# The last row tile's 20 rows on three groups of partitions, three chunks' products issued together

## The chip, the cores and the metric

The kernel runs on one core of one Trainium2 chip. The metric is device time in microseconds (us), lower is better. A core has TensorE (PE in the profile; PEld are its weight loads), VectorE (DVE), ScalarE (ACT), GpSimd (POOL), the queue engine SyncE (SP) and 16 DMA engines. PE contracts over partitions: a product `matmul(acc, lhsT, rhs)` sums over the partitions of lhsT and rhs and writes the result to PSUM.

## The reference

Four graph layers work on 2708 nodes with 128 features each and one dense adjacency matrix of 2708 x 2708 (fp32, 29 MB), with a residual and a layer norm after each:

```python
# layer 0: neighbourhood mean, similarity of z, the 4 nearest are added to A
d = 1 / sqrt(sum(A, -1));  z = leaky_relu((d * (A @ (d * x))) @ W1 + b1)
S = exp(-dist(z, z) / 2), kept for the 4 nearest of each row;  A2 = S + A
x = layernorm(x + (d2 * (A2 @ (d2 * x))) @ W2 + b2)
# layer 1: attention
XW = x @ W;  den = exp(leaky_relu(s_row[:, None] + s_col[None, :]));  num = A @ den
x = layernorm(x + A @ ((den / num) @ XW))
# layer 2: normalised adjacency
x = layernorm(x + (dn * (A @ (dn * x))) @ W.T + b)
# layer 3: own features beside the neighbours' sum
x = layernorm(x + relu(concat([x, A @ x]) @ W.T + b))
```

A enters six times as the large operand. Each time the kernel passes over all of it, with the nodes as the contraction.

## The kernel before

A is stored transposed. A pass computes `acc[:, k] = sum over j of lhsT[j, :] * adjT[j, k]`. The 2708 rows j make T = 22 row tiles of 128; the last, tile 21 (`FULL`), has `LAST` = 20 rows. The columns k make C = 6 chunks of 512, 512, 512, 512, 384 and 276. Of the row tiles, S = 16 are streamed from memory in every pass, four to a panel, through a pool of three buffers; six (16 to 21) stay in SBUF in `res`. A chunk's sum is one PSUM bank.

Five of the six passes run through this helper (the operands are called y2, lc, mixed, y3 and xs; y2 and y3 share a buffer that the profile calls y):

```python
    def by_panels(weights, done, tick=None, ready=(), first=None, behind=None):
        ready = list(ready)
        for c in range(C):
            w = cw[c]
            acc = acc_tile()
            for n, i in enumerate(first if first and c == 0 else range(T)):
                if i < S:
                    if i % 4 == 0:
                        ...                                  # load the next panel
                    src = part[:, i % 4, :w]
                else:
                    src = res[: pw[i], i - S, cols[c]]       # pw[21] is 20
                lhsT = weights(i)
                nc.tensor.matmul(                            # L181 in the profile
                    acc[: lhsT.shape[-1], :w], lhsT=lhsT, rhs=src, start=(n == 0), stop=(n == T - 1 and tick is None)
                )
                if n == T - 1:
                    done(c, acc)
                if tick is not None:
                    tick()
```

`done` evacuates the sum and does the chunk's small work (bias, residual, norm, the next operand). The y2 pass also calls `tick`, which issues other work at given counts of products: the kernel gathers each node's four nearest rows with indirect DMAs on GpSimd (88 of them, `got`), sums them on VectorE (`near_sum`), and adds the sums to acc by a product with the identity (L580).

The first pass is written out on its own, since it runs while A is first read:

```python
        def add(c, i, src, first=False, last=False):
            nc.tensor.matmul(                                # L364 in the profile
                accs[c][:, : cw[c]], lhsT=y[: pw[i], i, :], rhs=src[: pw[i], : cw[c]], start=first, stop=last
            )
        ...
        def add_group(c, g, part, last=False):
            for i in chunk_tiles[g]:                         # group 5 holds tiles 19, 20 and 21
                add(c, i, part[:, i % 4, :] if i < S else resident(c, i), i == 0, last and i == chunk_tiles[g][-1])
                due.tick()
        ...
            rest(3, 4)
            add_group(*wait)                                 # chunk 5, group 5
            finish(5)
            rest(3, 5, True)
            finish(3)
            for c in (2, 1, 0): ...                          # each ends with its group 5
```

The order of the passes: the first pass (operand y), the similarity of z (PE and VectorE), the y2 pass, a ranking of the attention scores, the lc pass (its lhsT has 86 columns), the attention itself (L1008 and L937, rows gathered by indirect DMA into the panels' buffers), and then the passes on mixed, y3 and xs. In front of the xs pass stands a loop over the 22 tiles with a transpose (L1061) and a product with layer 3's own-feature weights (L1065); the scheduler weaves it into that pass's first chunk.

PSUM pools: six acc buffers up to the similarity stage, three after it.

Of the kernel before, what the change touches and what calls it, by code (L numbers as in the profile page):

```python
# [16 lines left out]
P = 128  # L17
# [33 lines left out]
def kernel(  # L51
# [16 lines left out]
    nc = tc.nc  # L68
    N, D = x.shape
    assert D == P  # L70
    T = (N + P - 1) // P
# [13 lines left out]
    cw = [b - a for a, b in zip(starts, [*starts[1:], N])]  # L85
    cols = [slice(a, a + w) for a, w in zip(starts, cw)]

    chunk_tiles = [range(a // P, (a + w + P - 1) // P) for a, w in zip(starts, cw)]

    const = ctx.enter_context(tc.tile_pool(name="const", bufs=1))  # L90
# [57 lines left out]
    def load_panel(g, c, pool=stream):  # L148
# [5 lines left out]
        )  # L154
        return s

    def by_panels(weights, done, tick=None, ready=(), first=None, behind=None):

        ready = list(ready)
        for c in range(C):
            w = cw[c]
            acc = acc_tile()
            for n, i in enumerate(first if first and c == 0 else range(T)):
                if i < S:
                    if i % 4 == 0:
                        if ready:
                            part = ready.pop(0)  # L170
                        elif behind is not None:
                            with tc.issue_after(behind):
                                part = load_panel(i // 4, c)
                            behind = None
                        else:
                            part = load_panel(i // 4, c)
                    src = part[:, i % 4, :w]
                else:
                    src = res[: pw[i], i - S, cols[c]]
                lhsT = weights(i)  # L180
                nc.tensor.matmul(  # L181
                    acc[: lhsT.shape[-1], :w], lhsT=lhsT, rhs=src, start=(n == 0), stop=(n == T - 1 and tick is None)
                )
                if n == T - 1:
                    done(c, acc)
                if tick is not None:
                    tick()

# [5 lines left out]
        return done  # L194

    def rows_of(y):
        return lambda i: y[: pw[i], i, :]

    def inv_sqrt(dst, src):
        nc.scalar.activation(dst, src, AF.Sqrt)  # L200
# [100 lines left out]
    with tc.tile_pool(name="knn", bufs=1) as knn:  # L301
# [59 lines left out]
        accs = [acc_tile() for _ in range(C)]  # L361

        def add(c, i, src, first=False, last=False):
            nc.tensor.matmul(  # L364
                accs[c][:, : cw[c]], lhsT=y[: pw[i], i, :], rhs=src[: pw[i], : cw[c]], start=first, stop=last
            )

        def resident(c, i):
            return res[:, i - S, cols[c]]
# [1 line left out]
        due = Due()  # L371

        def add_group(c, g, part, last=False):
            for i in chunk_tiles[g]:
                add(c, i, part[:, i % 4, :] if i < S else resident(c, i), i == 0, last and i == chunk_tiles[g][-1])
                due.tick()

        def finish(c):
# [12 lines left out]
        with (  # L391
            tc.tile_pool(name="load", bufs=4) as load,
            tc.tile_pool(name="degp", bufs=2) as degp,
            tc.manual_schedule(engines={nc.tensor.engine}),
        ):
            wait = None
            for c in range(C):
                w = cw[c]
                load_x(chunk_tiles[c])
                parts = [load_panel(g, c, load if g < G - 1 else stream) for g in range(G)]  # L400
                nc.sync.dma_start(
                    res[:, : FULL - S, cols[c]],
                    adjT[S * P : FULL * P, cols[c]].rearrange("(t p) k -> p t k", p=P),
                )
                if LAST:
                    nc.sync.dma_start(res[:LAST, FULL - S, cols[c]], adjT[FULL * P :, cols[c]])
                both = degp.tile([P, 2, CW], F32, tag="both", name="both")
                nc.vector.tensor_add(both[:, :, :w], parts[0][:, :2, :w], parts[0][:, 2:, :w])
                more = [part[:, n : n + 2, :w] for part in parts[1:] for n in (0, 2)]
                more += [res[:, n : n + 2, cols[c]] for n in range(0, RES, 2)]  # L410
                for m in more:
                    nc.vector.tensor_add(both[:, :, :w], both[:, :, :w], m)
                nc.vector.tensor_add(both[:, 0, :w], both[:, 0, :w], both[:, 1, :w])

                for g in range(min(c, G)):
                    add_group(c, g, parts[g])
                    if wait is not None:
                        add_group(*wait)
                        wait = None
                if c == C - 1:  # L420
                    add_group(c, G, None)
                ts = chunk_tiles[c]
                dps = mis_tile()
                for k, t in enumerate(ts):
                    nc.tensor.matmul(
                        dps[: pw[t], k : k + 1], lhsT=both[:, 0, k * P : k * P + pw[t]], rhs=ones, start=True, stop=True
                    )
                full = sum(pw[t] == P for t in ts)
                t0, t1 = ts[0], ts[-1] + 1
                nc.vector.tensor_copy(deg[:, t0 : t0 + full], dps[:, :full])  # L430
                if t0 + full < t1:
                    nc.vector.tensor_copy(deg[:LAST, t0 + full : t1], dps[:LAST, full : full + 1])
                inv_sqrt(dinv[:, t0:t1], deg[:, t0:t1])
                scale_rows(y, xs, dinv, ts)
                wait = (c, c, parts[c] if c < G else None, c == C - 1)
                if c == C - 2:
                    w1_sb = load_const(w1, D, "w1")
                    w2_sb = load_const(w2, D, "w2")
                    wa_sb = load_const(w_att, D, "w_att")
                    wl_sb = load_const(w_lap_t, D, "w_lap")  # L440
                    wx_sb = load_const(w_cat_t[:D, :], D, "w_cat_x")
                    wh_sb = load_const(w_cat_t[D:, :], D, "w_cat_h")
                    b1_sb = load_rows(b1, D, "b1")
                    b2_sb = load_rows(b2, D, "b2")
                    bl_sb = load_rows(b_lap, D, "b_lap")
                    bc_sb = load_rows(b_cat, D, "b_cat")
                    a_sb = load_rows(a_att, 2 * D, "a_att")


            def rest(c, g, end=False):  # L450
                add_group(c, g, load_panel(g, c) if g < G else None, end)

            assert (C, G) == (6, 4)
            rest(3, 4)
            add_group(*wait)
            finish(5)
            rest(3, 5, True)
            finish(3)
            for c in (2, 1, 0):
                for g in range(c + 1, C):  # L460
                    if (c, g) == (1, 4):
                        rest(4, 5, True)
                        finish(4)
                    rest(c, g, g == C - 1)
                finish(c)
            due.flush()
# [15 lines left out]
        def weigh(ts):  # L482
# [14 lines left out]
            if t1 < T:  # L497
                nc.gpsimd.tensor_mul(  # L498
                    y2[:, t0:t1, :], xs[:, t0:t1, :], d2inv[:, t0:t1, None].to_broadcast([P, t1 - t0, D])
                )  # L500
            else:
                scale_rows(y2, xs, d2inv, ts)
            full = min(t1, FULL)
            queue = nc.gpsimd if t1 < T else nc.sync
            ins = queue.dma_start(
# [180 lines left out]
        at(near_at[t], sum_near, t)  # L686

    def end_pass2(c, acc):
        n = max(T * (c + 1), near_at[chunk_tiles[c][-1]] + 3)
        ts = chunk_tiles[c]  # L690

        def finish():
# [42 lines left out]

    with tc.manual_schedule(engines={nc.tensor.engine, nc.vector.engine, nc.scalar.engine}):
        by_panels(
            rows_of(y2), end_pass2, due.tick, ready, [*range(S - 4), *range(S, T - 2), *range(S - 4, S), T - 2, T - 1], written
        )
        due.flush()  # L740
    late.close()
# [7 lines left out]
    with tc.tile_pool(name="rank", bufs=1) as rank:  # L749
# [72 lines left out]
        with tc.manual_schedule(engines={nc.vector.engine}):  # L822
            for t0, t1 in ((0, 4), (4, half_t), (half_t, T)):
# [10 lines left out]
                for side, (op, v) in enumerate(((ALU.is_gt, e_r), (ALU.is_lt, f_r))):  # L834
                    sel = rtile([half_t, NB], "sel", BF16)
                    nc.vector.tensor_tensor(sel[:, :n, :], blk_g, iota_g, op=op)
                    nc.vector.tensor_mul(lc[:, t0:t1, :, side], sel[:, :n, :], v[:, t0:t1, None].to_broadcast([P, n, NB]))  # L837

        for t0, t1 in halves:
            n = t1 - t0  # L840
# [75 lines left out]
            if c == 3:  # L916
                listed()

        by_panels(lambda i: lc[: pw[i], i, :, :].rearrange("p b s -> p (b s)"), end_carry)
        gb = on_all("gb", r_row)  # L920

    def mix(w, q, num, col, haccs, pool):
# [97 lines left out]
    for t in range(T):  # L1020
        p = pw[t]
        pt = mis_tile()
        nc.tensor.transpose(pt[:p, :D], mT[:, t * P : t * P + p], ident)  # L1023
        nc.vector.tensor_scalar_mul(mixed[:p, t, :], pt[:p, :D], f_out[:p, t : t + 1])


    nc.vector.tensor_scalar_add(dinv, deg, DEG_EPS)
# [3 lines left out]
    def end_layer1(c, ts):  # L1031
# [5 lines left out]
        normalize(ts, xs)  # L1037
        for t in ts:
            nc.scalar.mul(y3[: pw[t], t, :], xs[: pw[t], t, :], dinv[: pw[t], t : t + 1])
            nc.gpsimd.tensor_add(xs[: pw[t], t, :], xs[: pw[t], t, :], bl_sb[: pw[t]])  # L1040

    by_panels(rows_of(mixed), into_hT(end_layer1))
# [4 lines left out]
    def end_layer2(c, ts):  # L1047
        for t in ts:
# [3 lines left out]
                xs[:p, t, :], po[:p, :D], dinv[:p, t : t + 1], xs[:p, t, :], op0=ALU.mult, op1=ALU.add  # L1052
            )
        normalize(ts, xs)

    by_panels(rows_of(y3), into_hT(end_layer2))

# [61 lines left out]
```

## Time and profile before

| | |
|---|---|
| time, median of 3 runs | 1134.08 us (1127.51 to 1134.82) |
| span of the profiled run | 1132.0 us |
| instructions | 10737 |
| DMA | 193.89 MB, mean 171 GB/s |

The page gives the busy time of each engine, the span in 40 slices, and groups of instructions. A group's row reads: line, engine, operation, output <- inputs, partitions contracted * output partitions, size, count, busy time and mean length, idle time before. The products of the 20 rows are groups of their own when shapes are kept apart:

```profile
L181 PE MATMUL acc<-res,y 20*128 20x512 f32 x16 | 9.0, 640 | 0.0
L364 PE MATMUL acc<-res,y 20*128 20x512 f32 x8 | 4.5, 640 | 0.0
L181 PE MATMUL acc<-res,mixed 20*128 20x512 f32 x8 | 4.5, 640 | 0.0
L181 PE MATMUL acc<-res,xs 20*128 20x512 f32 x8 | 4.5, 640 | 0.0
L181 PE MATMUL acc<-res,lc 20*86 20x512 f32 x8 | 4.3, 622 | 0.0
```

One fp32 product leaves two records, so x8 are the four chunks of 512 columns of one pass. Records overlap, since a product's end is modelled: what a product takes is read from one start to the next, not from the mean length.

### The profile page before, as it was taken

What the parts mean: (1) busy time and instruction counts of PE and PEld (TensorE: products, weight loads), DVE (VectorE), ACT (ScalarE), POOL (GpSimd) and SP (SyncE); (2) the same over time, 40 slices, a digit from 0 to 9 for tenths busy, and PEclk for the clock granted to TensorE, in tenths of its full rate; (3) what the DMA queues carried; (4) which work ended last, traced back from release to release, by engine and by line L of the source; (5) the groups of instructions that cost most, each with busy time, mean ns of one, the idle gap of its engine ahead of it and who ended that gap; (6) DMA issues with size and microseconds to landing.
All of it is one profiled execution on the core that took longest, in us unless ns stands there. A gap on an engine that the chain in (4) does not pass through costs nothing.

```text
span 1132.0 us, 10737 instructions
## 1 busy us (share of the span) xinstructions
PE 1061.9 (94%) x3495; PEld 496.7 (44%) x3495; DVE 643.0 (57%) x1381; ACT 302.9 (27%) x557; POOL 300.4 (27%) x296
## 2 busy tenths in 40 slices
PE   0899999999999994999899999998999999999997
PEld 0346444444344563333433333333444644565444
DVE  5985439999726678502189999998311211223132
ACT  0000135555302344000065666664100100011000
POOL 4000000000377772773255655561010100000000
PEclk9999999999999996999999999999999999999999
DMA  9996330000386660696635534554475776565743
GB/s 346 335 321 224 112 111 1 1 0 1 121 281 201 208 205 26 195 294 226 206 109 151 172 104 119 161 174 151 150 237 180 219 226 220 166 212 168 250 157 112
DMA packets 110246, 193.89 MB, mean 171 GB/s; under 512 B 14157, under 2 KB 47107, under 8 KB 109927
## 3 DMA queue, kind: packets, MB, share of 16 engines
q1 hardware_dynamic: 91046, 151.12, 40.7%
q0 software_dynamic: 19136, 42.01, 12.1%
q8 instruction: 29, 0.48, 0.2%
q14 instruction: 35, 0.28, 0.1%
HBM read 217.20 MB, written 4.30 MB: 196 GB/s over the span
## 4 chain that ended last, share of the span: by engine, by line
PE 36%; issue 6%; POOL 4%; DMA 3%; DVE 1%; ACT 0%; POOLq 0%; DVEq 0%
PE acc L181 26%; PE hacc L937 4%; PE num L1008 4%; POOL rows L995 4%; DMA rows<-in_adjT,slot_i 2%; DMA part<-in_adjT 1%; PE mis L231 1%; DMA rows<-carry 0%; PE mis L1065 0%; PE mis L1023 0%; PE mis L1061 0%; POOLq L995 0%; PE mis L1035 0%; DVE err L931 0%; ACT mT L1013 0%
## 5 line engine op out<-in xcount | busy, mean ns | idle before, releaser
L181 PE MATMUL acc<-part,y 128*128 128x512 f32 (+2 forms) x384 | 155.9, 548 | 2.2 <-DMA part<-in_adjT 1.7
L995 POOL DMA_INDIRECT rows<-in_adjT,slot_i x86 | 120.4, 1400 | 107.6 <-PE num L1008 79.7
L1008 PE MATMUL num<-rows,lw 128*64 128x512 f32 (+2 forms) x516 | 117.1, 558 | 5.3 <-DMA rows<-carry 2.1
L937 PE MATMUL hacc<-err,xws 128*128 128x512 f32 (+3 forms) x264 | 112.1, 561 | 2.2 <-DVE err L932 1.8
L535 PE MATMUL acc<-zT,z 128*128 128x512 f32 (+4 forms) x264 | 108.6, 558 | 0.0
L563 POOL DMA_INDIRECT got<-y_rows,where x88 | 93.9, 1067 | 29.6 <-issue 10.1
L181 PEld LDWEIGHTS acc<-part,y 128*128 128x128 f32 x384 | 69.3, 190 | 67.3 <-issue 57.5
L930 DVE TENSOR_TENSOR err<-inv,num 128x1024 f32<-128x1024 f32 (+1 forms) x88 | 74.3, 855 | 26.1 <-DMA rows<-in_adjT,slot_i 20.0
L926 ACT ACTIVATE inv<-num 128x1024 f32<-128x1024 f32 (+1 forms) x88 | 64.4, 735 | 86.9 <-PE num L1008 84.3
L536 ACT COPY key<-acc 128x512 f32<-128x512 f32 (+3 forms) x132 | 70.3, 535 | 59.6 <-issue 29.8
L364 PE MATMUL acc<-part,y 128*128 128x512 f32 (+2 forms) x192 | 82.5, 582 | 2.3 <-DVE y L205 2.2
L937 PEld LDWEIGHTS hacc<-err,xws 128*128 128x128 f32 (+1 forms) x264 | 46.5, 189 | 79.7 <-issue 42.3
L181 PE MATMUL acc<-part,lc 128*86 128x512 f32 (+2 forms) x192 | 76.5, 554 | 2.5 <-DVE lc L837 2.5
L181 PE MATMUL acc<-part,xs 128*128 128x512 f32 (+2 forms) x192 | 77.9, 546 | 0.3 <-DMA part<-in_adjT 0.3
L932 DVE SCALAR_TENSOR_TENSOR err<-gb,g_inv,err 128x1024 f32<-128x1024 f32 (+1 forms) x88 | 77.1, 917 | 0.0
L498 POOL TENSOR_TENSOR y<-xs,d2inv 128x2176 f32<-128x2176 f32 (+1 forms) x2 | 4.6, 2324 | 271.7 <-ACT d2inv L496 271.6
L181 PE MATMUL acc<-part,mixed 128*128 128x512 f32 (+2 forms) x192 | 75.6, 546 | 0.2 <-DMA part<-in_adjT 0.2
L535 PEld LDWEIGHTS acc<-zT,z 128*128 128x128 f32 (+1 forms) x264 | 47.5, 188 | 55.4 <-issue 50.1
L931 DVE SCALAR_TENSOR_TENSOR err<-err,inv 128x1024 f32<-128x1024 f32 (+1 forms) x88 | 71.8, 857 | 0.0
L192 ACT COPY hT<-acc 128x512 f32<-128x512 f32 (+2 forms) x18 | 9.6, 536 | 231.0 <-PE acc L181 231.0
L537 DVE MAX8 near<-key 128x8 f32<-128x2708 f32 (+1 forms) x22 | 65.5, 2979 | 4.8 <-ACT key L536 4.8
L927 ACT ACTIVATE inv<-inv 128x1024 f32<-128x1024 f32 (+1 forms) x88 | 67.2, 768 | 2.6
(233 smaller groups left out, 1231.3 us busy)
## 6 DMA issues: line engine op xcount, KB each, us to landing
part<-in_adjT SPq DMA_DIRECT2D x102, 1024.0 KB
part<-in_adjT SPq DMA_DIRECT2D x24, 768.0 KB
part<-in_adjT SPq DMA_DIRECT2D x24, 552.0 KB
res<-in_adjT SPq DMA_DIRECT2D x4, 1280.0 KB
got<-y_rows,where POOLq DMA_INDIRECT x88
rows<-in_adjT,slot_i POOLq DMA_INDIRECT x86
rows<-carry SPq DMA_DIRECT2D x86, 10.6 KB
xws<-by_rank POOLq DMA_DIRECT2D x1, 1365.0 KB
```

The costliest lines, as they stand in the source:

```text
L181: nc.tensor.matmul(acc[: lhsT.shape[-1], :w], lhsT=lhsT, rhs=src, start=(n == 0), stop=(n == T - 1 and tick is None))
L364: nc.tensor.matmul(accs[c][:, : cw[c]], lhsT=y[: pw[i], i, :], rhs=src[: pw[i], : cw[c]], start=first, stop=last)
L535: nc.tensor.matmul(pks[c][:p, : cw[c]], lhsT=z2[:, :p], rhs=zT[:, cs], start=False, stop=True)
L536: nc.scalar.copy(key[:p, cs], pks[c][:p, : cw[c]])
L563: nc.gpsimd.indirect_dma_start(out=got[:p, :], out_offset=None, in_=y2_rows[:, :], in_offset=bass.IndirectOffsetOnAxis(ap=where[:p, t, k : ...
L927: nc.scalar.activation(inv[:p], inv[:p], AF.Exp, scale=-1.0)
L930: nc.vector.tensor_mul(err[:p], inv[:p], num[:p, :w])
L931: nc.vector.scalar_tensor_tensor(err[:p], err[:p], 2.0, inv[:p], op0=ALU.subtract, op1=ALU.mult)
L932: nc.vector.scalar_tensor_tensor(err[:p], gb[:p, col : col + w], g_inv[:p, q : q + 1], err[:p], op0=ALU.max, op1=ALU.mult)
L937: nc.tensor.matmul(haccs[:, o:e], lhsT=xws[:p, q, :D], rhs=err[:p, o:e], start=(q == 0), stop=(q == NQ - 1))
L995: nc.gpsimd.indirect_dma_start(out=rows[:KC, n, :], out_offset=None, in_=adj_half[:, :], in_offset=bass.IndirectOffsetOnAxis(ap=slot_i[h][ ...
L1008: nc.tensor.matmul(num[n * BJ : n * BJ + bw[b], o:e], lhsT=lw[:, b, : bw[b]], rhs=rows[:, n, c0 + o : c0 + e], start=True, stop=True,)
```

## The change

The 20 rows of tile 21 use 20 of PE's 128 rows. The change puts the resident 20 rows of chunk c on the partitions from 32 x (c mod 3), and keeps the operand's 20 rows on all three groups of partitions (two small copies by `spread`). The products of three neighbouring chunks then use different rows of PE, and they are issued one after the other: those of chunks 0, 1 and 2 at the end of chunk 0, and those of chunks 3, 4 and 5 at the end of chunk 3. The other chunks begin with a sum that already holds the 20 rows, and end with tile 20. In the first pass all six stand together. The aim is that PE works on three of them at a time and changes its shape less often.

```diff
+    def few(c):
+        g = c % GROUPS * 32
+        return slice(g, g + LAST)
+
+    def spread(rows, engine=None):
+
+        for g in range(1, GROUPS):
+            (engine or nc.scalar.copy)(rows[few(g)], rows[few(0)])
+
     def by_panels(weights, done, tick=None, ready=(), first=None, behind=None):
         ready = list(ready)
+        accs = {}
+
+        def product(c, i, src, w):
+            lhsT = weights(i)[few(c) if i == FULL else slice(None)]
+            start = c not in accs
+            if start:
+                accs[c] = acc_tile()
+            stop = tick is None and i == (FULL if c % GROUPS == 0 else FULL - 1)
+            nc.tensor.matmul(accs[c][: lhsT.shape[-1], :w], lhsT=lhsT, rhs=src, start=start, stop=stop)
+
         for c in range(C):
             w = cw[c]
-            acc = acc_tile()
-            for n, i in enumerate(first if first and c == 0 else range(T)):
+            for i in [*(first if first and c == 0 else range(FULL)), *([FULL] if c % GROUPS == 0 else [])]:
+                if i == FULL:
+                    for n in range(c, c + GROUPS):
+                        product(n, i, res[few(n), i - S, cols[n]], cw[n])
+                    done(c, accs[c])
+                    for _ in range(GROUPS if tick is not None else 0):
+                        tick()
+                    continue
...
-                    src = res[: pw[i], i - S, cols[c]]
-                lhsT = weights(i)
-                nc.tensor.matmul(
-                    acc[: lhsT.shape[-1], :w], lhsT=lhsT, rhs=src, start=(n == 0), stop=(n == T - 1 and tick is None)
-                )
-                if n == T - 1:
-                    done(c, acc)
+                    src = res[:, i - S, cols[c]]
+                product(c, i, src, w)
+                if i == FULL - 1 and c % GROUPS:
+                    done(c, accs[c])
                 if tick is not None:
                     tick()
...
+        def add_few():
+            for c in range(C):
+                nc.tensor.matmul(
+                    accs[c][:, : cw[c]], lhsT=y[few(c), FULL, :], rhs=res[few(c), FULL - S, cols[c]],
+                    start=False, stop=False,
+                )
                 due.tick()
...
-                    nc.sync.dma_start(res[:LAST, FULL - S, cols[c]], adjT[FULL * P :, cols[c]])
+                    nc.sync.dma_start(res[few(c), FULL - S, cols[c]], adjT[FULL * P :, cols[c]])
...
             rest(3, 4)
+            add_few()
             add_group(*wait)
```

`spread` is called on row tile 21 of each operand as soon as it is there: y, y2, lc, mixed, y3 and xs. In the first pass `add_group` skips tile 21. In the y2 pass a chunk's follow-up work is timed from the running count of products, since the counts at the chunks' ends have moved. The rest of the diff is indices.

More of the change, by code (lines that the diff above doesn't have):

```diff
@@ L86 @@
     cols = [slice(a, a + w) for a, w in zip(starts, cw)]
+    assert 0 < LAST <= 32
+    GROUPS = 3
+    def few(c):
+        g = c % GROUPS * 32
+        return slice(g, g + LAST)
     chunk_tiles = [range(a // P, (a + w + P - 1) // P) for a, w in zip(starts, cw)]
@@ L196, in rows_of @@
     def rows_of(y):
-        return lambda i: y[: pw[i], i, :]
+        return lambda i: y[:, i, :]
     def inv_sqrt(dst, src):
@@ L363, in add @@
         def add(c, i, src, first=False, last=False):
-            nc.tensor.matmul(
-                accs[c][:, : cw[c]], lhsT=y[: pw[i], i, :], rhs=src[: pw[i], : cw[c]], start=first, stop=last
-            )
+            nc.tensor.matmul(accs[c][:, : cw[c]], lhsT=y[:, i, :], rhs=src[:, : cw[c]], start=first, stop=last)
         def resident(c, i):
@@ L373, in add_group @@
         def add_group(c, g, part, last=False):
-            for i in chunk_tiles[g]:
-                add(c, i, part[:, i % 4, :] if i < S else resident(c, i), i == 0, last and i == chunk_tiles[g][-1])
+            ts = [i for i in chunk_tiles[g] if i < FULL]
+            for i in ts:
+                add(c, i, part[:, i % 4, :] if i < S else resident(c, i), i == 0, last and i == ts[-1])
+                due.tick()
+        def add_few():
[4 more added lines that the diff above has]
+                )
                 due.tick()
@@ L434 @@
                 scale_rows(y, xs, dinv, ts)
+                if c == C - 1:
+                    spread(y[:, FULL, :])
                 wait = (c, c, parts[c] if c < G else None, c == C - 1)
@@ L502, in weigh @@
                 scale_rows(y2, xs, d2inv, ts)
+                spread(y2[:, FULL, :])
             full = min(t1, FULL)
@@ L688, in end_pass2 @@
     def end_pass2(c, acc):
-        n = max(T * (c + 1), near_at[chunk_tiles[c][-1]] + 3)
+        n = max(due.n + 1, near_at[chunk_tiles[c][-1]] + 3)
         ts = chunk_tiles[c]
@@ L737 @@
         by_panels(
-            rows_of(y2), end_pass2, due.tick, ready, [*range(S - 4), *range(S, T - 2), *range(S - 4, S), T - 2, T - 1], written
+            rows_of(y2), end_pass2, due.tick, ready, [*range(S - 4), *range(S, T - 2), *range(S - 4, S), T - 2], written
         )
@@ L837 @@
                     nc.vector.tensor_mul(lc[:, t0:t1, :, side], sel[:, :n, :], v[:, t0:t1, None].to_broadcast([P, n, NB]))
+        spread(lc[:, FULL, :, :])
         for t0, t1 in halves:
@@ L917, in end_carry @@
                 listed()
-        by_panels(lambda i: lc[: pw[i], i, :, :].rearrange("p b s -> p (b s)"), end_carry)
+        by_panels(lambda i: lc[:, i, :, :].rearrange("p b s -> p (b s)"), end_carry)
         gb = on_all("gb", r_row)
@@ L1024 @@
         nc.vector.tensor_scalar_mul(mixed[:p, t, :], pt[:p, :D], f_out[:p, t : t + 1])
+    spread(mixed[:, FULL, :])
     nc.vector.tensor_scalar_add(dinv, deg, DEG_EPS)
@@ L1039, in end_layer1 @@
             nc.scalar.mul(y3[: pw[t], t, :], xs[: pw[t], t, :], dinv[: pw[t], t : t + 1])
+            if t == FULL:
+                spread(y3[:, t, :])
             nc.gpsimd.tensor_add(xs[: pw[t], t, :], xs[: pw[t], t, :], bl_sb[: pw[t]])
@@ L1054, in end_layer2 @@
         normalize(ts, xs)
+        if ts[-1] == FULL:
+            spread(xs[:, FULL, :])
     by_panels(rows_of(y3), into_hT(end_layer2))
```

## The prediction

> **What bounds the kernel now.** I read the page first, for engines and chain, then the busy time of each engine by stretch, then PE's timeline at the end of a row of products, and last the waits where PE is not alone.
>
> ```profile
> PE 1061.9 (94%) x3495; PEld 496.7 (44%) x3495; DVE 643.0 (57%) x1381; ACT 302.9 (27%) x557; POOL 300.4 (27%) x296
> PE 36%; issue 6%; POOL 4%; DMA 3%; DVE 1%; ACT 0%; POOLq 0%; DVEq 0%
> ```
>
> PE is busy 94% of the span. But an average over six passes with different limits says nothing of one pass, so the stretches matter:
>
> ```profile
> 300.00:427.00 127.00, 120.71 (x504) 65.39 (x502) 70.98 (x261) 32.60 (x72) 95.61 (x91) 1.00 0.68 221
> 454.00:559.00 105.00, 104.97 (x270) 40.79 (x270) 27.30 (x95) 3.93 (x10) 55.57 (x54) 0.98 0.75 238
> 797.00:1009.00 212.00, 211.51 (x591) 104.41 (x590) 38.30 (x190) 16.98 (x46) 9.77 (x22) 1.00 0.65 205
> 1038.00:1125.00 87.00, 86.26 (x255) 44.24 (x253) 20.59 (x105) 3.65 (x10) 0.00 (x0) 1.00 0.58 185
> ```
>
> The columns are the stretch, its length, then busy time and count of PE, PEld, DVE, ACT and POOL, PE's clock, DMA share and GB/s. The passes on lc (454 to 559), mixed and y3 (797 to 1009) and xs (1009 to 1125) are PE from end to end with DMA at 0.58 to 0.75. The pass on y2 (300 to 427) has POOL at 95.61 of 127 and PE idle for over 6 us; that one needs its own look. The first pass is PE without a gap from about 89 to 156 us.
>
> What a 20-row product costs, from PE's timeline in the last pass:
>
> ```profile
> 1038.43 13.04 PE L181 MATMUL acc<-part,xs 128*128 128x512 f32 x30
> 1051.31 5.51 PE L181 MATMUL acc<-res,xs 128*128 128x512 f32 x12
> 1056.74 1.12 PE L181 MATMUL acc<-part,xs 128*128 128x512 f32 x2
> 1057.70 1.05 PE L231 MATMUL mis<-w_cat_h,hT 128*128 128x128 f32 x8
> ```
>
> Each fp32 product leaves two records. From start to start, 30 records take 1051.31 - 1038.43 = 12.88 us: 0.429 a record, 0.859 a product. The 12 records on res (five full products and the 20-row one) take 5.43 us; less 10 x 0.429 that is 1.14 for the 20-row product, and the full product after it takes 0.96 instead of 0.86. So **a 20-row product costs 1.24 us: 0.86 to stream 512 columns, as much as 128 rows take, and 0.38 for going into its shape and out again.** By the same streaming rate it is 0.64 + 0.38 = 1.02 for 384 columns and 0.46 + 0.38 = 0.84 for 276. A pass of six chunks pays 4 x 1.24 + 1.02 + 0.84 = 6.82 us for row tile 21.
>
> [...] The kernel before has no row groups, but it has two column groups, and there the trace shows full overlap, in fp32[...]:
>
> ```profile
> 706.16 2.54 PE L937 MATMUL hacc<-err,xws 128*128 128x512 f32 x6
> 708.63 2.50 PE L1008 MATMUL num<-rows,lw 128*64 128x330 f32 x12
> 711.05 2.54 PE L937 MATMUL hacc<-err,xws 128*128 128x512 f32 x6
> ```
>
> Six records of full width take 2.47 us (706.16 to 708.63), and twelve of 64 columns, of the same lengths and in pairs, take 2.42. [...]
>
> **The change part by part.** It adds twelve ACT copies of 20 partitions, two for each of y, y2, lc, mixed, y3 and xs, of 128 columns or fewer; ACT copies of 128 columns take 266 ns here (xT), so about 0.3 us each. They follow the last tile of an operand; the first product that reads them stands at the end of the next pass's first chunk, some 18 us later. Only in the first pass is this close: y of tile 21 is written on DVE by 102.03, two copies end by about 102.7, and PE still has three full products from 100.67 (to 103.3) ahead of it. No wait expected. The loads of the 20 rows only change partitions.
>
> What it removes is PE time. Three products of one triple should cost what one costs, 1.24 us, the widest of them setting the length. Per pass:
> - First pass: all six stand together, one entry and exit and two rounds of 0.86: 2.10 instead of 6.82, **4.7 us**. PE is the limit there, and the similarity stage behind it, untouched in itself, starts and ends that much earlier; so do the gathers of the y2 pass.
> - y2 pass: see the rivals, **0**.
> - lc pass: lhsT has 86 columns and the trace reads slightly lower (1.19 by the same subtraction). Chunks 1, 2 and 4 lose their product: 1.19 + 1.19 + 0.97 = **3.3 us**. Chunk 5's also goes, but what follows waits for gathered rows:
>
> ```profile
> 552.83 1.11 POOL L995 DMA_INDIRECT rows<-in_adjT,slot_i  x1 [11.31 <-PE acc L181]
> 560.23 1.04 PE L1008 MATMUL num<-rows,lw 128*64 128x512 f32 x2 [0.93 <-DMA rows<-in_adjT,slot_i]
> ```
>
> The gather starts when PE gives back a panel's buffer, in mid chunk 5, and PE already waits 0.93 us for it; a shorter tail of chunk 5 only makes that wait longer.
> - mixed and y3: 6.82 - 2 x 1.24 = 4.34 each, **8.7 us**. The panels have room: the only DMA wait is about 0.3 us in each chunk 5, set by a buffer's release and the load's 3.9 us, and it stays.
> - xs: here the instruction order of the built program counts. Transposes and own-row products of the last layer are woven into the first chunk, one after every product. They also fall between the three of the triple, as they do now around the single 20-row product:
>
> ```profile
> 1034.22 0.27 PE L1061 MATMUL mis<-ident,xs 128*128 128x128 f32 x1
> 1034.42 1.12 PE L181 MATMUL acc<-res,xs 20*128 20x512 f32 x2
> 1035.47 0.49 PE L1065 MATMUL mis<-w_cat_x,xT 128*128 128x128 f32 x2
> ```
>
> So that triple stays three single visits and gains nothing. Only the second triple gains: 1.24 + 1.02 + 0.84 - 1.24 = **1.9 us**.
>
> The own-rows stage from 560 to 797 has no row tile 21 as a contraction of panels and only moves with its start.
>
> Sum: 4.7 + 0 + 3.3 + 8.7 + 1.9 = 18.6 us. I take off half a microsecond for starts that are not quite together: 18. From 1134.1 that is 1116 us, -1.6%.
>
> **The rivals.** (a) The y2 pass gains too. Against it:
>
> ```profile
> 306.76 1.12 POOL L563 DMA_INDIRECT got<-y_rows,where  x1 [3.10 <-DMA y_rows<-y]
> ...
> 426.17 0.96 POOL L563 DMA_INDIRECT got<-y_rows,where  x1 [0.31 <-issue]
> ```
> ```profile
> 414.76 0.49 PE L580 MATMUL acc<-ident,near_sum 128*128 128x128 f32 x2 [1.45 <-DVE near_sum L571]
> 426.77 0.49 PE L580 MATMUL acc<-ident,near_sum 128*128 128x128 f32 x2 [1.53 <-DVE near_sum L571]
> 428.99 0.61 PE L580 MATMUL acc<-ident,near_sum 20*128 20x20 f32 x2 [1.73 <-DVE near_sum L571]
> ```
>
> 88 gathers follow each other every 1.3 us or so whatever PE does, and PE waits for their sums at the end. Time saved on PE turns into a longer wait. Were it to gain all the same, the time would be 1112.
>
> (b) [...]with two records per product, the second of one could only overlap the first of the next. A triple of 512 then takes four rounds of 0.43 instead of two. Each triple costs 0.6 to 0.85 more, and about 12 us are left: 1122. The column groups speak against it. (c) Row groups do not overlap at all: only the spared entries and exits remain, 0.38 for four of six visits per pass, about 7 us: 1127. (d) A new wait: three acc banks must be free at the end of chunks 0 and 3, and the pool has three. Before, each was evacuated at least a chunk earlier; in the lc pass, the evacuation of chunk 2 on DVE stands behind a DMA (done at 520 us, needed at about 530 by today's clock). A wait there would cost some 3 us.
>
> **Range and chances.** Full overlap gets about 0.8, which with run-to-run spread (before: 1127.5 to 1134.8) gives 1111 to 1119; (b), (c) and (d) pull the upper end to 1126, (a) and a low reading the lower to 1109. More than 2% means under 1111.4, more than 22 us: it needs the y2 pass or noise, 0.16. Slower by 2% would need a stall that nothing here shows: 0.01.
>
> **What would show it.** Right: 20-row records starting together by threes, one entry per triple; passes of mixed and y3 shorter by 4.3 each, of lc by 3.3, of xs by 1.9; the gather of y2's pass starting 4.7 earlier and lasting as long, with PE's waits for near_sum up by about 4. Wrong: 20-row records 0.43 us apart within a triple (b, c), PE waiting on ACT or DVE at the end of chunks 0 or 3 (d), or the y2 pass itself shorter (a).

## The result and the profile after

The changed kernel takes 1118.55 us (median of 4 runs, 1114.82 to 1121.06), the kernel before beside it 1133.05 (4 runs, 1127.51 to 1134.82). The ratio is 0.9878, with a 95% interval of 0.9829 to 0.9927: about 14 us gained, less than 2%. The span of the profiled run falls from 1132.0 to 1119.4 us.

The page after, first the engines' busy time, then PE's clock in 40 slices, then the chain that ended last by engine:

```profile
PE 1044.2 (93%) x3495; PEld 494.5 (44%) x3495; DVE 642.7 (57%) x1381; ACT 306.1 (27%) x569; POOL 299.4 (27%) x296
PEclk9999999999999995999999999998999999998999
PE 51%; issue 4%; DMA 4%; DVE 2%; POOL 1%; ACT 1%; POOLq 0%; DVEq 0%; ACTq 0%
```

The number of products is the same (x3495), ACT has the twelve copies more (557 to 569), and PE is busy 17.7 us less while the span falls by only 12.6: some of the time won on PE came back as waiting. The chain still runs mostly over PE (51% where it was 36%, POOL 1% where it was 4%) and names no new bound. The last 8 in the clock row, four slices from the end, is new and lies in the xs pass (the 8 before it is the end of the own-rows stage).

The busy time by stretch shows where PE is no longer full. The columns are as in the prediction; the stretches are the passes on lc, mixed, y3 and xs:

```profile
445.50:548.50 103.00, 101.32 (x270) 40.35 (x270) 27.33 (x95) 4.83 (x13) 55.96 (x54) 0.98 0.76 244
787.00:890.00 103.00, 101.41 (x289) 50.58 (x288) 18.59 (x94) 11.97 (x33) 8.49 (x19) 1.00 0.63 203
890.00:994.50 104.50, 102.94 (x306) 52.58 (x305) 20.52 (x100) 5.88 (x18) 1.27 (x3) 1.00 0.65 212
994.50:1119.40 124.90, 117.52 (x380) 62.58 (x379) 33.30 (x158) 11.35 (x38) 0.00 (x0) 0.96 0.54 175
```

Over mixed and y3 PE had been busy 211.51 of 212 us; now it idles over 1.5 us in each. In the xs pass its clock reads 0.96.

Stage by stage, from the first instruction of a stage to the first of the next unless the row says otherwise, in the two profiled runs (the rows do not cover the whole span):

| stage | before | after | difference | predicted |
|---|---|---|---|---|
| first pass | 64.67 | 60.48 | -4.19 | -4.7 |
| similarity | 139.18 | 137.49 | -1.69 | 0 |
| y2 pass, first to last gather | 119.41 | 118.46 | -0.95 | 0 |
| lc pass, to the first row gather | 98.82 | 96.39 | -2.43 | -3.3 |
| own-rows stage, first to last product | 229.14 | 231.71 | +2.57 | 0 |
| mixed | 105.34 | 102.80 | -2.54 | -4.34 |
| y3 | 107.39 | 104.63 | -2.76 | -4.34 |
| xs, to the end | 123.47 | 125.02 | +1.55 | -1.9 |

The load phase ahead of these rows is another 1.88 us shorter after. The own-rows stage is not touched by the change; over the fourteen profiled runs of this study it scatters from 227 to 235 us, and the load phase from 89.3 to 93.1. I draw nothing from either. The similarity stage's 1.69 is half of a 3.4 us stretch at clock 0.50 (168.0 to 171.4 us) that, of these two runs, only the one before had.

**The triples overlap.** PE's timeline where the first pass has all six 20-row products, and at the first triple of mixed:

```profile
98.79 2.84 PE L392 MATMUL acc<-res,y 128*128 128x512 f32 x6
101.56 1.98 PE L407 MATMUL acc<-res,y 20*128 20x512 f32 x12
103.47 2.91 PE L392 MATMUL acc<-res,y 128*128 128x276 f32 x8
```
```profile
801.40 5.52 PE L186 MATMUL acc<-res,mixed 128*128 128x512 f32 x16
807.63 0.66 PE L1076 MATMUL mis<-ident,hT 128*128 128x128 f32 x4 [0.71 <-ACT hT L220]
```

Twelve records take 1.91 us from the first start to the next full product (101.56 to 103.47). In sequence they would stream for 4.5, an estimate from the prediction's 0.86, 0.64 and 0.46. In mixed, ten records of full products and six of the triple run from 801.40 to 807.63; less the idle 0.71 and 10 x 0.429 that leaves 1.23 for three products. In the single records the first halves of a triple start 6 to 7 ns apart, the second halves 0.53 us later, again together.

**The wait that was not foreseen** stands in the second of these lines. PE is through with the triple and idles 0.71 us, because its next instruction, the chunk's transposes of hT, waits for ACT to copy the finished sum out of PSUM. Before, the next chunk's first product stood between (in the prediction's timeline of the last pass, the line at 1056.74 between the 20-row product and the L231 products). PE's waits from 780 to 1000 us, as total, times and longest, and below them those of the kernel before over the same two passes (790 to 1010 us):

```profile
PE mis L1076 <- ACT hT L220: 1.4, 2, 0.7
PE mis L1063 <- ACT mT L1053: 1.4, 1, 1.4
PE mis L259 <- ACT hT L220: 1.3, 2, 0.7
PE acc L186 <- DMA part<-in_adjT: 0.4, 2, 0.2
```
```profile
PE mis L1023 <- ACT mT L1013: 1.4, 1, 1.4
PE acc L181 <- DMA part<-in_adjT: 0.5, 2, 0.3
```

The wait for mT, ahead of mixed, and those for panels are old and no longer than before, so contention for memory is not what costs here. Those for hT are new. Four triples, four waits of 0.7 us. ACT was free ahead of the copy, so it is the copy's own time, laid bare:

```profile
806.99 0.58 ACT L220 COPY hT<-acc 128x512 f32<-128x512 f32 x1 [16.82 <-issue]
```

**The y2 pass** did what was predicted. The first and last gather, and PE's waits there:

```profile
298.99 1.12 POOL L602 DMA_INDIRECT got<-y_rows,where  x1 [3.08 <-DMA y_rows<-y]
...
417.44 1.07 POOL L602 DMA_INDIRECT got<-y_rows,where  x1 [0.30 <-issue]
```
```profile
PE acc L619 <- DVE near_sum L610: 7.2, 3, 3.9
```

The gathers start 7.8 us earlier (4.2 from the first pass, 1.9 from the load phase, 1.7 from the similarity stage) and last as long within 1 us; PE waits 7.2 us for their sums where it waited 4.7. What PE saves here it spends waiting.

**The lc pass** has a new wait for a panel in its last chunk, and then still waits for the gathered rows:

```profile
539.50 5.81 PE L186 MATMUL acc<-part,lc 128*86 128x276 f32 x24 [0.81 <-DMA part<-in_adjT]
545.15 2.49 PE L186 MATMUL acc<-res,lc 128*86 128x276 f32 x10
548.73 1.04 PE L1048 MATMUL num<-rows,lw 128*64 128x512 f32 x2 [1.08 <-DMA rows<-carry]
```

**The xs pass**, where the first chunk ends:

```profile
1020.11 1.12 PE L186 MATMUL acc<-res,xs 20*128 20x512 f32 x2
1021.16 0.49 PE L1110 MATMUL mis<-w_cat_x,xT 128*128 128x128 f32 x2
1021.58 0.23 PE L1106 MATMUL mis<-ident,xs 20*128 20x20 f32 x1
1021.58 1.12 PE L186 MATMUL acc<-res,xs 20*128 20x512 f32 x2
1022.63 0.40 PE L1110 MATMUL mis<-w_cat_x,xT 128*20 128x128 f32 x2
1022.96 1.95 PE L186 MATMUL acc<-res,xs 20*128 20x512 f32 x2
1024.84 2.08 PE L259 MATMUL mis<-w_cat_h,hT 128*128 128x128 f32 x8
```

Woven work breaks the triple into three visits, as predicted. But the third visit takes 1.95 us and the eight records behind it 2.08, where before they took 1.05: PE's clock reads 0.50 here, for 6.8 us from 1023.1.

### The profile page after: what moved, and what is told of

Read it like the earlier page. It is cut to its first block, busy times and chain, and to the rows that moved or that the text cites. A ratio compares the mean times of both kernels' runs of the same rounds, so it can differ in the third digit from the quotient of the medians.

```text
span 1119.4 us, 10743 instructions
## 1 busy us (share of the span) xinstructions
PE 1044.2 (93%) x3495; PEld 494.5 (44%) x3495; DVE 642.7 (57%) x1381; ACT 306.1 (27%) x569; POOL 299.4 (27%) x296
## 4 chain that ended last, share of the span: by engine, by line
PE 51%; issue 4%; DMA 4%; DVE 2%; POOL 1%; ACT 1%; POOLq 0%; DVEq 0%; ACTq 0%
PE acc L186 32%; PE hacc L977 8%; PE num L1048 8%; DMA rows<-in_adjT,slot_i 2%; DMA part<-in_adjT 1%; PE mis L259 1%; POOL rows L1035 1%; DVE mask L692 1%; PE mis L1110 0%; PE mis L1063 0%; DMA got<-y_rows,where 0%; ACT junk L710 0%; ACT hT L220 0%; PE mis L1076 0%; DVE mask L697 0%
```

## The experiments

Theory: the triples gain in full, and what is missing against the prediction is (1) the evacuation laid bare behind each triple and (2) in xs the broken triple with its clock. Rivals: the triples overlap only in part; the grouping is not what gains, but only fewer changes of shape; the lost time is contention for memory.

The runs were made on different chips. On two of them (those of runs e4_same to e8_early_tall and of f_after to e9_gb_out) the kernel before takes 1173 to 1174 us. In all profiles from these two, the y2 pass and the ranking together take 193 to 200 us instead of 159, with 53 to 67 us of it at half clock instead of 23 to 30; why these chips differ stays open. So each ratio is to the kernel before on the same chip, taken without runs more than 1.5% above the fastest of their kernel, and stages are compared outside these two.

**The changed kernel once more**, unedited.

> The changed kernel once more, beside the others on the same chip. Every theory expects 1118.5 us within 3, ratio about 0.988. Theory (clock): the granted clock falls to half again in the xs pass, at its first chunk's end, where the three 20-row products stand apart. Rival (chance): the dip sits elsewhere or is missing.

Ratio 0.9876 (0.9832 to 0.9921), 1123.05 us beside 1137.17. Mixed and y3 are 102.55 and 104.88, as in the first profile. But xs takes 121.92 us, 3.1 less, with the same broken triple and without half clock (1.00 from 1000 to 1080 us). So the broken triple alone does not bring the clock down.

**The triple one place earlier**: it comes ahead of tile 20, so the chunk ends with a full product, as its neighbours do.

```diff
-            stop = tick is None and i == (FULL if c % GROUPS == 0 else FULL - 1)
+            stop = tick is None and i == FULL - 1
...
+            if tick is None and c % GROUPS == 0:
+                order[-2:] = [FULL, FULL - 1]
```

> The three products of a triple are issued one place earlier, before tile 20 instead of after it, in the passes on lc, mixed, y3 and xs; the follow-up work of chunks 0 and 3 then hangs on a full product. Theory (order): PE waited 0.7 us behind each triple because the follow-up stands directly behind it and needs the evacuated sum; a product of the next chunk now stands between, as in the kernel before. 5 or 6 waits of 0.74 vanish: about 4 us less than the changed kernel, 1114.5, and no idle PE in front of the transposes of mixed. Rival (late sums): three sums written at once come late, so the wait stays in front of the next products: 1118.5.

PE's timeline at the same place as above, and its waits from 780 to 1000 us:

```profile
804.17 5.72 PE L186 MATMUL acc<-res,mixed 128*128 128x512 f32 x16
809.72 1.02 PE L186 MATMUL acc<-part,mixed 128*128 128x512 f32 x2
810.61 0.66 PE L1081 MATMUL mis<-ident,hT 128*128 128x128 f32 x4
```
```profile
PE hacc L982 <- DVE err L977: 1.8, 1, 1.8
PE mis L1068 <- ACT mT L1058: 1.4, 1, 1.4
PE acc L186 <- DMA part<-in_adjT: 0.7, 2, 0.4
```

The next chunk's first product (x2 at 809.72) stands again between the sum and its transposes, and the waits for hT are gone from the list. Mixed takes 101.95 and y3 103.38. Over all profiles with the triple at the end (six: after, a_again, e2_whole, e7_first_undone, f_after, e9_gb_out) the means are 102.73 and 104.74, over all with it one place earlier (five: e1_early, e3_both, e8_early_tall, f_early, f_early_tall) 101.66 and 103.27: 1.1 and 1.5 us, close to two waits of 0.7 in each pass. Ratio 0.9817 (0.9781 to 0.9853), median 1117.40 us.

**The triple of xs kept whole**, issued after the last woven product; then both edits together.

```diff
+                    with tc.issue_after(after) if after is not None and c == 0 else ExitStack():
...
-        nc.tensor.matmul(po[:p, :D], lhsT=xT[:, :p], rhs=wx_sb, start=True, stop=True)
+        woven = nc.tensor.matmul(po[:p, :D], lhsT=xT[:, :p], rhs=wx_sb, start=True, stop=True).ins
```

> As the changed kernel, but in the xs pass the first triple is ordered behind the last of the woven own-row products, so that its three products stand together. Theory (clock and visits): two visits of 1.24 us go, the new wait behind the triple of 0.7 comes, and the half clock after 1012 us, about 3.4 us, goes too because PE is not three times in a row at 20 rows: 1113 to 1114. Rival (chance dip): only the visits count, 1116.5 to 1117, and a dip may stand there as before.

> Both changes: triples one place earlier, and the first triple of the xs pass whole. The theories of order and of clock together expect 4.4 + 2.5 + 3.4 less than the changed kernel: 1108 to 1109. With only the waits right: 1114. With only the visits and the waits: 1111.5.

Ratios 0.9857 (0.9822 to 0.9893) and 0.9829 (0.9792 to 0.9867). Both gain less than was expected: against the changed kernel on the same chip the medians are 3.2 us lower where 5 were expected, and 5.8 where 10 were. With the triple whole xs still takes 124.70 us, again with 6.8 us at half clock (0.91 on average from 1000 to 1040 us); with both edits 120.88 and no half clock there (1.00). The whole triple does not gain its full 2.5 us (two visits of 1.24), as the own-row products now lack something to stand between them. In the timeline with both edits:

```profile
1021.06 0.49 PE L1116 MATMUL mis<-w_cat_x,xT 128*128 128x128 f32 x2 [0.41 <-ACT xT L1114]
1021.38 0.27 PE L1112 MATMUL mis<-ident,xs 128*128 128x128 f32 x1
1022.07 0.49 PE L1116 MATMUL mis<-w_cat_x,xT 128*128 128x128 f32 x2 [0.41 <-ACT xT L1114]
1022.49 0.23 PE L1112 MATMUL mis<-ident,xs 20*128 20x20 f32 x1
1023.04 0.40 PE L1116 MATMUL mis<-w_cat_x,xT 128*20 128x128 f32 x2 [0.32 <-ACT xT L1114]
1023.36 2.19 PE L186 MATMUL acc<-res,xs 20*128 20x512 f32 x8
```

Three waits on ACT, 1.14 us together, take back nearly half of what the whole triple spares. That the clock dips with a whole triple (e2) and not with a broken one (a_again) rules out the visits as such; the last section has what the runs show of it.

**The same order, but one row group for all**: nothing can overlap.

```diff
     def few(c):
-        g = c % GROUPS * 32
-        return slice(g, g + LAST)
+        return slice(0, LAST)
...
     def spread(rows, engine=None):
-        for g in range(1, GROUPS):
-            (engine or nc.scalar.copy)(rows[few(g)], rows[few(0)])
+        return
```

> As the changed kernel, with the same order of instructions, but the 20 rows of all chunks lie on the first group of partitions, so that the products of a triple stand together and cannot overlap. Theory (overlap): a triple of 512 columns takes 2.58 + 0.38 instead of 1.24, the second one 1.1 more, the first pass 2.8 more; in mixed and y3 the 0.7 us wait behind each triple vanishes, although the follow-up still stands directly behind it, since the first sum is evacuated under the other two products: mixed and y3 each 1.4 longer, in all 7 to 9 us over the changed kernel, near 1127. Rival (shape): the gain came from fewer changes of shape alone: no longer than the changed kernel.

Ratio 1.0001 (0.9980 to 1.0021): all of the gain is gone. The loss of some 14 us is nearly twice the 7 to 9 expected; the stages below say how much of it is the overlap. PE's timeline at the first triple of mixed:

```profile
859.16 7.22 PE L184 MATMUL acc<-res,mixed 128*128 128x512 f32 x16
866.32 0.66 PE L1074 MATMUL mis<-ident,hT 128*128 128x128 f32 x4
```

From 859.16 to 866.32, less 10 x 0.429, three products take 2.87 us instead of 1.23. The wait for hT is absent: with three products in a row, the third hides the copy of the first sum. So the order fits products that do not overlap, and the overlap itself exposes the wait; mixed and y3 come out 1.2 and 1.3 us above the means with the triple at the end, and still 1.4 us each below the kernel before. The first pass takes 66.65 instead of 60.48, of which 3.4, by estimate, is half of a half-clock stretch of 6.8 us directly behind its six products. The lc pass is 12 us longer than in f_after. PE waits 5.9 us for panels there instead of 0.4, and 12.0 us of it run at half clock instead of 4.7, which is worth about 3.6, an estimate (half the difference); so this run says nothing exact of lc, and its ratio overstates what the overlap is worth.

**The kernel before with the 20 rows filled up with zeros to 128**: no grouping, and no change of shape either.

```diff
-                    src = res[: pw[i], i - S, cols[c]]
+                    src = res[:, i - S, cols[c]]
...
-        return lambda i: y[: pw[i], i, :]
+        return lambda i: y[:, i, :]
...
+    nc.gpsimd.memset(mixed[:, FULL, :], 0.0)
...
+    nc.gpsimd.memset(y3[:, FULL, :], 0.0)
```

> The kernel before, but the product of row tile 21 contracts all 128 partitions, 108 of them zero, in every chunk: no change of PE's shape, nothing grouped. Theory (shape): 0.38 us less for each 20-row product: 2.2 in the first pass, 1.6 in that on lc, 2.3 in each of mixed, y3 and xs, 0 in y2: 10 to 11 us less than before, about 1122, most of the gain of the grouped kernel. Rival (overlap alone): a product of 20 rows costs no more than one of 128 and only grouping pays: 1133, the same as before.

Ratio 0.9934 (0.9911 to 0.9957). PE's timeline at the end of mixed's first chunk:

```profile
864.02 5.31 PE L181 MATMUL acc<-res,mixed 128*128 128x512 f32 x12
869.17 1.02 PE L181 MATMUL acc<-part,mixed 128*128 128x512 f32 x2
```

Twelve records take 5.15 us, 12 x 0.429 exactly: the way into the shape and out is gone, and nothing else. Mixed, y3 and xs are 2.2, 1.9 and 1.9 us shorter than before (six visits by 0.38 would be 2.3), the first pass 1.75. So about half of the gain (by the ratios a bit over, with wide intervals) needs no row groups at all. The other part needs the overlap: without it, in e4, mixed and y3 keep only the 1.4 us that the spared shape changes account for.

**The first pass undone**: each chunk's 20-row product back in its own place, all else as changed (`add_few()` goes; `add_group` issues tile 21 with `few(c)`).

> The changed kernel with the first pass as before: its six 20-row products stand apart again, each behind its chunk. Theory: the 4.2 us that the first pass lost pass through the similarity stage unchanged, so this one takes 4 us more than the changed kernel, 1122.5. Rival: the similarity stage is limited by something that starts at the same time anyway: 1118.5.

The first pass is back at 64.67 us, and the y2 pass starts 4.2 us later after the load phase than in f_after (201.26 us instead of 197.09): the similarity stage passes the gain on in full. The ratio is 0.9925 (0.9897 to 0.9953), half a per cent worse than the changed kernel's on other chips. This fits a gain that reaches the end, but the changed kernel was not run on this chip, and the two intervals just touch.

**The triples one place earlier, and in xs's first three chunks no triple but single products of full height**, in the place of the 20-row ones:

```diff
+            one = tall and c < GROUPS
+            if one and c:
+                order.append(FULL)
...
+                if i == FULL and one:
+                    nc.tensor.matmul(
+                        accs[c][:, :w], lhsT=weights(i), rhs=res[:, i - S, cols[c]], start=False, stop=False
+                    )
+                    continue
```

> As e1 (triples one place earlier), and in the xs pass the products of row tile 21 in chunks 0 to 2 are full-height, one in its own chunk, instead of a triple that the woven work breaks up. Theory (shape): three times 0.38 less than e1, about 1 us, ratio to before 0.981; xs pass 1 us shorter than in the changed kernel without a clock dip, plus 0.7 for its second triple. Rival (chance): the difference drowns in the clock's dips, ratio as e1.

Ratio 0.9847 (0.9819 to 0.9876), not the expected 0.981; xs 120.69 us without half clock. Then the changed kernel, e1 and this one together on another chip:

> The changed kernel again, as the yardstick of this call: ratio 0.988. If the half clock in the xs pass comes from its three separate 20-row products, it stands there again at about 1023 us; if it is chance, in about half of the runs.

> Triples one place earlier, beside the changed kernel on the same chip: mixed and y3 1 us shorter each, lc and the second triple of xs 0 to 1 us; 3 to 4 us less than the changed kernel, ratio to before 0.982 to 0.985. Rival: the gain of the first comparison was drift of the chip; then 0.988.

> Triples one place earlier and full-height products in the first three chunks of the xs pass: 4 to 5 us less than the changed kernel, ratio to before 0.981 to 0.984, no half clock in the xs pass before its end. Rival: no better than the early triples alone.

| run | ratio to before | mixed | y3 | xs |
|---|---|---|---|---|
| f_after | 0.9875 (0.9848 to 0.9901) | 102.96 | 104.68 | 125.07 |
| f_early | 0.9858 (0.9823 to 0.9893) | 102.11 | 103.26 | 122.84 |
| f_early_tall | 0.9826 (0.9797 to 0.9855) | 101.03 | 103.21 | 120.56 |

The stages repeat. In the whole time the gain of the earlier triple is not certain, and the 3 to 4 us expected of f_early did not show. Its ratio is the lower one on both chips (0.9817 beside 0.9876, 0.9858 beside 0.9875), but the intervals overlap, and its medians are 5.7 us below the changed kernel's on one chip and 1.9 above on the other (there the untouched own-rows stage happened to take 6.6 us more in the profiled run). The last version has the best medians on its chips, 1152.61 beside 1158.29 for the changed kernel, but the intervals still touch.

**lc without the broadcast load of `gb`** (1354 KB), which might fall on the last panels. The kernel leaves that load out, and the attention that follows computes with ones in its place.

```diff
-        gb = on_all("gb", r_row)
+        gb = big.tile([P, N], F32, tag="hT", name="gb")
+        nc.gpsimd.memset(gb, 1.0)
```

> The changed kernel without the broadcast load of gb (a constant is written instead, so the attention's result is another; its time can be read). Theory (shared DMA): PE's new wait of 0.5 to 1 us for a panel in chunk 5 of the lc pass comes from that load of 1.4 MB, which falls on the last panels because PE is there earlier; without it the wait is gone and the pass up to the first row gather takes 95.5 instead of 96.3. Rival (fewer resident products): the panels had less time because chunk 4 has one product fewer; the wait stays.

This is a single run. PE's wait for a panel in lc is 0.2 us, where f_after on the same chip has 0.4, and the stage 95.95 against 96.46. But f_early_tall, with the load, also waits only 0.2. This is inconclusive: whether the load causes the wait stays open.

## Why the prediction was right, and where its steps were not

The total of 1118.55 lies 2.5 us above the predicted 1116, inside the range. Against the kernel before beside it, 14.5 us were gained of the 18 forecast. By its own steps:

- **"Three products of one triple should cost what one costs, 1.24 us"**: right; 1.23 in mixed, and by the single records 2.11 for the six of the first pass against a predicted 2.10. That row groups would overlap was an estimate, carried over from the column groups of the kernel before. The half microsecond taken off for starts that are not quite together was not needed. Rivals (b) and (c) fell with the records that start 6 to 7 ns apart, and with e4, where three in sequence take 2.87. Rival (d), a wait for an acc bank, is nowhere in the waits.
- **The 0.38 us of shape change**: right, shown by e6, where filling up with zeros takes away just that. What PE does in this time was not shown.
- **y2 at 0**: right; rival (a) fell. Waits for near_sum rose by 2.5 rather than "about 4".
- **Mixed and y3 at 4.34 each**: the step that failed. The sum counted what PE spares and not what comes behind it. The overlapped triple is too short to hide the copy of the first sum, so 0.7 us per triple, 1.4 per pass, come back as a wait; 2.5 and 2.8 are left. With the wait removed, the means of y3 come to 4.1 and of mixed to 3.7.
- **First pass at 4.7**: the stage gained 4.2. By the single records the six products went to 2.11 us as predicted, but from 6.57 and not from 6.82: the one of 384 columns and the last one had something other than a full product behind them, and paid less for leaving their shape (0.93 us instead of 1.02, and 1.03 instead of 1.24). The 3-row product of the next stage, which had shared the last one's change of shape, now pays 0.1 us of its own. That places 0.35 of the missing 0.5; the rest I did not trace. The run filled up with zeros, where nothing overlaps, misses as much in this pass (1.75 of 6 x 0.38 = 2.28), so the gap lies in the changes of shape and not in the overlap.
- **lc at 3.3**: 2.4. A wait of 0.81 us for a panel, which the kernel before did not have in that place, takes most of the difference. The prediction looked for room in the panels in mixed and y3, but not here. What causes the wait stays open.
- **xs at 1.9**: the broken triple was foreseen. Without half clock the pass gains 1.55 (a_again), with it it loses 1.55. The prediction had no term for PE's clock.

So the term sum of 18.6 was 5.1 us too large over these five passes (13.5 by the after column, with a_again's xs). Against the median difference of 14.5 this leaves 1 us, well within the spread of the untouched stages. So close a fit is partly luck: with the xs pass of the run after itself the five passes gain only 10.4.

## What to carry to other kernels

Where products overlap and an operation gets shorter, look at what the next instruction on that engine waits for: a copy that was hidden behind the long version can be laid bare by the short one, and one independent product placed between takes the wait away. A short contraction costs its change of shape (0.38 us here) besides its streaming, so filling it up with zeros to full height is the cheap first step (here about half of the gain), and row groups are the second. Read the clock where narrow products stand, also in a pass in which PE is busy throughout: here 6.8 us at half clock cost the xs pass 3.1 us (see below).

## What the runs showed of the hardware

**Half clock without an idle PE.** In the changed kernel's xs pass PE, by its busy time, is full throughout three neighbouring stretches of 3.4 us:

```profile
1016.30:1019.70 3.40, 3.40 (x16) 1.96 (x16) 0.88 (x3) 0.80 (x3) 0.00 (x0) 1.00 0.60 231
1019.70:1023.10 3.40, 3.40 (x14) 1.39 (x13) 0.62 (x3) 1.02 (x3) 0.00 (x0) 1.00 0.00 0
1023.10:1026.50 3.40, 3.40 (x10) 1.90 (x11) 0.94 (x4) 0.00 (x0) 0.00 (x0) 0.50 0.00 0
```

The clock column falls to 0.50 right behind the stretch from 1019.7 to 1023.1. In that one, by the timeline of the xs pass above, 20-row products take 2.24 of the 3.40 us: 1.05 each from 1020.11 and from 1021.58 to the next product of 128 rows, and the first 0.14 of the one from 1022.96. So PE's busy time alone did not keep the clock up here. The clock over the end of xs's first chunk in other runs:

| run | 20-row products there | clock, stretch |
|---|---|---|
| before | one | 1.00, 1009 to 1080 us |
| after | three, apart | 0.91, 1000 to 1040 us |
| a_again | three, apart | 1.00, 1000 to 1080 us |
| e2_whole | three, together | 0.91, 1000 to 1040 us |
| e3_both | three, together, one place earlier | 1.00, 1000 to 1080 us |
| e7_first_undone | three, apart | 1.00, 1000 to 1080 us |
| f_early | three, one place earlier | 0.50, 1065.8 to 1069.2 us |

All runs here with half clock have three 20-row products in this place, but not all with three have it. The same kernel fell to half clock in one run (after) and not in another (a_again), which is worth 3.1 us of xs (125.02 beside 121.92). In f_after xs took 125.07, as long as in the first of these two. In e4's first pass, too, 6.8 us at half clock stand directly behind six 20-row products. That it is the rows at work that count, and not PE's busy time, is my reading of this after the fact; no run was made to test it, and what decides between two runs of one kernel was not shown. Only that the full-height version has no half clock in xs before its end was expected before it ran; it had none both times, with xs at 120.69 and 120.56 us.

**Overlap in fp32.** Each fp32 product's two records interleave with those of its neighbours in the triple; nothing of the order that rival (b) assumed is to be seen. Where the widths differ, the second halves even start in the reverse of the program's order. In the first pass's second triple the first halves start at 102.526, 102.532 and 102.539 us (512, 384 and 276 columns), the second halves at 102.955, 102.855 and 102.771, which is 0.429, 0.323 and 0.232 us after their own first halves: the streaming time of each width at the rate read above (0.429 for 512). Of the ends the traces show nothing, since they are modelled.
